# Layer 3's attention: five VectorE exponential tiles a block instead of four, the block's end in five pieces, and statistics' steps placed anew

## The chip, the cores and the metric

The kernel is one launch on one core of a Trainium2 chip. The metric is the device time in microseconds of that core; the median of the runs shown stands for a kernel. The engines are named PE (TensorE), DVE (VectorE), ACT (ScalarE), POOL (GpSimd) and SP (the queue that issues DMAs). [...]

## The reference

Four layers are applied to an image `x` of shape (2, 128, 64, 64), each to a group-normalised copy and added back: `x = x + layer(_gn(x))`. Layer 0 is an attention with four heads and depthwise convolutions, layer 1 a set of convolutions with a correlation, layer 2 a product of spectra (a two-dimensional real FFT, a quaternion product with weights per frequency, the inverse FFT). Layer 3, in which most of the change lies, is a plain attention of 8 heads with 16 channels each over 4096 positions:

```python
q = proj(wq, bq); k = proj(wk, bk); v = proj(wv, bv)      # (B, 8, 16, 4096)
a = jnp.einsum('bhcq,bhck->bhqk', q, k) / jnp.sqrt(jnp.float32(C))
a = jax.nn.softmax(a, axis=-1)
o = jnp.einsum('bhqk,bhck->bhcq', a, v)
```

All of it is computed in fp32.

## The kernel before

**Layer 3.** The work is cut into four groups: two images, and for each two sets of four heads (`b`, `t`). A group has eight blocks of 512 queries (`qb`), and a block has 32 iterations, one for each tile of 128 keys (`kt`). An iteration (`scores`) writes the scores of four heads by PE (L2316) into two PSUM tiles of [128, 2, 512], one for each pair of heads (`p` is 0 or 1). These come from a pool of three, two banks each[...]. One exponential instruction turns a PSUM tile into a tile of weights in SBUF: usually ACT's (L2330). For the tiles named in `BY_VECTOR`, DVE computes the exponential itself, with a chain of eight instructions (`exponentials`): `exp_i` reads the scores (L2272), two integer steps split exponent and mantissa (L2277, L2280), four terms of a polynomial (L2288) and the last term with the power of two make the weights (L2292). The chain is a generator, and the loop advances it by one piece an iteration, ahead of that iteration's scores, so DVE's order is fixed by the loop.

The products with the values (`multiply`, L2339) follow three iterations behind the scores (`LAG`), so those of a block's last key tile are issued in iteration 2 of the next block. `ORDER` says at which place of the sum each key tile is multiplied: a tile of DVE's comes some places later than its own. After the last one, `done` ends the block on DVE: a transpose of the accumulator (L2362), reciprocals of the sums (L2366), the product (L2367), a transpose back (L2369), the sum with the residual (L2370) and the stores.

While a group runs, the keys, queries and values of the next are made in the same loop (`queries_and_keys` in four pieces at the iterations of `KEYS`, `values` at iteration `VALUES`). In a usual block of the first three groups this is one chunk of queries and keys and one of values: PE's matmuls are L2197 and L2243, DVE's parts L2200 to L2223 and L2250. A group that is behind catches up at `MORE_KEYS`. Small steps (`bound`, the statistics of the next image, `folded`) stand at the iterations of `SMALL`. In the very first block of the layer, the first group's own keys and values are made, a chunk at every second iteration.

`_in_order` keeps each engine's instructions in program order. The tile framework assigns the buffers of a pool and places the semaphores.

**Statistics.** `_stats_steps` computes the group statistics of an image in eleven steps: eight `bn_stats` on DVE (L1444), their aggregation (L1447), a small matmul with the mean and three short DVE instructions (L1450 to L1459), and a small matmul with the variance, ended by a power on POOL (L1462, L1429, L1430). Layer 1 takes them in turn with its last chunks, each of which has a matmul series (L710), a sum (L721) and some of the DVE taps (L662). Layer 2 takes them in its last stage (`turned_back`, `added`; L1158 to L1175).

**Layer 2's start.** `placed` spreads the transformed rows of an image over the partitions (`copied`, L960 on ACT and L962 on DVE; even rows by ACT, odd rows by DVE). The second half of the weights' product (L1024) needs all rows of the mirrored part.

Of the kernel before, what the change touches and what calls it, by code (L numbers as in the profile page):

```python
# [18 lines left out]
CH = 512  # L19
# [512 lines left out]
def _layer1(ctx, tc, X, a, cst, here=None, there=None, consts=None):  # L532
# [216 lines left out]
    for b in range(B):  # L749
        for c in range(NCH):  # L750
            if c in (0, 2):
                z = on_tiles(g[b], t2[b], c // 2)
            ps = combined(t9[b], t2[b], c)

            for x in ready:
                added(*x)
            ready = [(b, c * CH, ps)]
            if c in (1, 3):
                ready.append((b, c // 2 * S // 2, z))
            some(rest, (4, 2, 4, 2, 3, 2, 2, 2)[c])  # L760
            some(steps, 2)
        if there is not None and b == 0:
            for x in ready:
                added(*x)
            ready = []
            steps = _stats_steps(nc, two, bank, X[:, 0, :], cst, mhalf, there)
# [36 lines left out]
def _layer2(ctx, tc, X, weights, cst, src, here=None, there=None, beside=None):  # L803
# [26 lines left out]
    with tc.tile_pool(name="l2_a", reuse_waits="tile", bufs=3) as ap, tc.tile_pool(  # L830
# [23 lines left out]
        scales = [st]  # L854
        shifts = [shifted(st)]
        if B > 1:
# [53 lines left out]
    with tc.tile_pool(name="l2_e", reuse_waits="tile", bufs=4) as ep, tc.tile_pool(  # L910
# [34 lines left out]

        def placed(kb, m, got, image, e, scalar):

            row = (m - 1) % 4  # L950
            s, row = (1, 3 - row) if image else (0, row)

            def copied(r, p, n=1):
                to = slice(32 * p, 32 * p + 32 * n)
                of = slice(32 * (r ^ p), 32 * (r ^ p) + 32 * n)
                sign = signs if n == 4 else float(SIGN2[r][p])
                out = e[to, row, :, 4 * r : 4 * r + 4].rearrange("p f (b c) -> p b f c", c=2)
                sign = sign[to, :] if n == 4 else sign
                if scalar:
                    nc.scalar.mul(out, got[of, :, s], sign)  # L960
                else:
                    nc.vector.tensor_scalar_mul(out, got[of, :, s], sign)  # L962

            copied(0, 0, 4)
            copied(2, 2, 2)
            copied(2, 0)
            copied(2, 1)
            yield
            for r in (1, 3):
                for p in range(4):  # L970
                    copied(r, p)
                yield
# [9 lines left out]

        def rows_in(kb, rows, places, es):

# [3 lines left out]
            yield  # L988
            yield from copies(kb, rows, gots, places, es)

        def copies(kb, rows, gots, places, es):
            for image in places:
                if es[image] is None:
                    es[image] = ep.tile([128, 4, 2 * PAIRS, 8 * B], F32, tag="e", name="e")
                yield from together(
                    *(
                        placed(kb, m, got, image, es[image], i % 2 == 0)
                        for i, (m, got) in enumerate(zip(rows, gots))
# [116 lines left out]
        for kb in range(BLOCKS2):  # L1115
# [10 lines left out]
            else:  # L1126
                later = side
                side, n = [copies(0, first[:2], gots[:2], (1,), e), rows_in(0, first[2:], (1,), e)], 8
            alongside(
# [18 lines left out]
    with tc.tile_pool(name="l2_c", reuse_waits="tile", bufs=3) as cp, tc.tile_pool(  # L1148
        name="l2_cps", reuse_waits="tile", bufs=4, space=PSUM
    ) as cps:  # L1150
        for b in range(B):
            xi = X[:, b, :].rearrange("p (h w) -> p h w", w=W)

            def turned_back(i):
                pt = cps.tile([128, CH], F32, tag="pt", name="ps_pt")
                for n in range(4):
# [5 lines left out]
                    )  # L1162
                for _ in range(2):
                    next(steps, None)
# [166 lines left out]
SMALL = (7, 9, 13, 15, 24, 28)  # L1331
BY_VECTOR = {(5, 1): 11, (12, 1): 18, (20, 1): 26, (27, 1): 31}

# [805 lines left out]
def _layer3(ctx, tc, X, l3, cst, out, worst, here, dram):  # L2139
# [129 lines left out]
    def exponentials(ps, out):  # L2269
# [17 lines left out]
        for n in EXP_TERMS[:-1]:  # L2287
            nc.vector.scalar_tensor_tensor(z, x, n, m, ALU.add, ALU.mult)  # L2288
            x = z
            yield  # L2290
        w = pp.tile([128, 2, CH], F32, tag="weights", name="weights")
# [6 lines left out]
    class Group:  # L2298

        def __init__(self, b, t, f, idle=0):  # L2300
            self.b, self.t, self.f, self.ac = b, t, f, None
            self.kept, self.q, self.k = {}, {}, {}
            self.vt = two.tile([128, NQT, 2, 3, 16], F32, tag="vt", name="vt")
# [4 lines left out]

    chain = [iter(())]

    def scores(g, qb, kt):
# [11 lines left out]
        for p in range(2):  # L2323
            g.weights[qb, kt, p] = w = []
            if (kt, p) in BY_VECTOR:
                chain[0] = exponentials(ps[p], w)
# [5 lines left out]
    def multiply(g, qb, at):  # L2332
        if at == 0:
            g.ac = acc()
        for j in range(4):

            i, kt = j % 2, ORDER[j // 2][at]
            (w,) = g.weights[qb, kt, j // 2]
# [7 lines left out]
        if at == NQT - 1:  # L2346
            done(g.b, g.t, qb, g.ac)

    def done(b, t, qb, ps):
# [12 lines left out]
        nc.vector.transpose(flat, ps)  # L2362
        r = two.tile([128, CH // 32], F32, tag="r", name="r")
        for j in range(4):
            rows = slice(32 * j, 32 * j + 32)
            nc.vector.reciprocal(r[rows, :], z[rows, :, 16 * (1 - j % 2)])  # L2366
        nc.vector.tensor_mul(z, z, r.unsqueeze(2).to_broadcast([128, CH // 32, 32]))  # L2367
        u = two.tile([128, CH], F32, tag="u", name="u", bufs=1)
        nc.vector.transpose(u, flat)  # L2369
        nc.vector.tensor_add(u, u, xs)  # L2370
        for at, rows in places:
            nc.sync.dma_start(out[b, rows, cols], u[at, :])

    def in_turn(*gens):
# [26 lines left out]
    def attended(g, early, others, following):  # L2401
# [19 lines left out]
        for n in range(NCH * NQT):  # L2421
# [3 lines left out]
            next(chain[0], None)  # L2425
            scores(g, qb, kt)
            waiting.append((g, qb, kt))
            if len(waiting) > LAG:
# [62 lines left out]
    for x in waiting:  # L2491
        multiply(*x)


# [32 lines left out]
def kernel(ctx, tc, a, out):  # L2527
# [4 lines left out]
    with tc.tile_pool(name="keep", bufs=1) as keep:  # L2532
        X, cst, eps5 = _inputs(tc, keep, a)

        worst = keep.tile([128, 1 + 2 * B], F32, name="worst")
        st = keep.tile([128, B + 2, 2], F32, name="st")
        rows_of_weights = _layer0(tc, X, a, cst, worst, st[:, :B], dram)
# [86 lines left out]
```

## Time and profile before

| | us |
|---|---|
| median of 3 runs | 4001.92 (4000.72 to 4008.1) |
| the profiled execution | 4003.18 |
| its span, first to last instruction | 4001.4 |
| busy PE / DVE / ACT in the span | 3853.4 / 3200.6 / 3243.5 |
| first scores of layer 3 | 2133.3 |

The page gives busy time, the span in slices, DMA, the chain that ended last, and groups of instructions as `line engine op out<-in xcount | busy, mean ns | idle before, releaser`. A timeline line is `start, length, engine, line, op, tiles`, with the idle time ahead of it and what ended that in brackets. Instructions on ACT and DVE overlap their neighbours a little, so a mean length is more than the distance of two starts; the ends of matmuls are modelled. Layer 3 takes 1867 us of the span, from 2133 to its end.

### The profile page before, as it was taken

What the parts mean: (1) busy time and instruction counts of PE and PEld (TensorE: products, weight loads), DVE (VectorE), ACT (ScalarE), POOL (GpSimd) and SP (SyncE); (2) the same over time, 40 slices, a digit from 0 to 9 for tenths busy, and PEclk for the clock granted to TensorE, in tenths of its full rate; (3) what the DMA queues carried; (4) which work ended last, traced back from release to release, by engine and by line L of the source; (5) the groups of instructions that cost most, each with busy time, mean ns of one, the idle gap of its engine ahead of it and who ended that gap; (6) DMA issues with size and microseconds to landing.
All of it is one profiled execution on the core that took longest, in us unless ns stands there. A gap on an engine that the chain in (4) does not pass through costs nothing.

```text
span 4001.4 us, 82144 instructions
## 1 busy us (share of the span) xinstructions
PE 3853.4 (96%) x35202; PEld 1313.9 (33%) x35202; DVE 3200.6 (80%) x3577; ACT 3243.5 (81%) x3948; POOL 86.2 (2%) x145
## 2 busy tenths in 40 slices
PE   7999999989999998998998999999999999999998
PEld 4511221353111124446664232232233222322222
DVE  6599999858999998996758777777777777776666
ACT  4499999736899983226645999999999999999998
POOL 1000000000000001000000000000000000000000
PEclk9999999999999999999998999999999999999999
DMA  1199960000000000004744110110002000110000
GB/s 51 23 200 185 187 106 2 1 2 2 2 2 2 2 2 13 6 19 199 280 199 150 32 32 25 53 46 31 26 27 72 30 27 25 44 47 6 6 6 5
DMA packets 193128, 217.59 MB, mean 54 GB/s; under 512 B 30441, under 2 KB 154345, under 8 KB 188658
## 3 DMA queue, kind: packets, MB, share of 16 engines
q1 hardware_dynamic: 192754, 212.25, 20.5%
q8 instruction: 278, 4.55, 0.5%
q14 instruction: 96, 0.79, 0.1%
HBM read 178.64 MB, written 98.57 MB: 69 GB/s over the span
## 4 chain that ended last, share of the span: by engine, by line
PE 78%; DVE 10%; issue 4%; ACT 2%; POOL 0%; SPq 0%; DMA 0%; ACTq 0%; POOLq 0%; DVEq 0%
PE ps_acc L2339 25%; PE ps_s L2316 19%; PE ps L1884 11%; PE ps L1892 11%; DVE X L662 3%; PE ps_z L1024 2%; PE ps_bank L710 2%; DVE sums L1915 2%; PE ps L1645 2%; DVE e L962 1%; PE ps_bank L681 1%; PE ps_bank L1078 1%; PE ps_acc L2197 1%; PE ps_acc L2243 1%; PE ps_pe L937 1%
## 5 line engine op out<-in xcount | busy, mean ns | idle before, releaser
L2330 ACT ACTIVATE weights<-ps_s 128x1024 f32<-128x1024 f32 x1920 | 1781.3, 1062 | 75.6 <-PE ps_s L2316 75.4
L2339 PE MATMUL ps_acc<-weights,vt 128*32 128x512 f32 x8192 | 1092.9, 605 | 0.0
L1915 DVE TENSOR_TENSOR sums<-sums,weights 128x2048 f32<-128x2048 f32 x384 | 854.2, 2283 | 3.5 <-ACT weights L1967 1.4
L2316 PE MATMUL ps_s<-q,k 64*128 64x512 f32 x4096 | 830.3, 469 | 3.7 <-DMA k<-stack 2.4
L1967 ACT ACTIVATE weights<-ps 128x1536 f32<-128x1536 f32 x512 | 740.6, 1447 | 6.9 <-PE ps L1892 6.9
L2316 PEld LDWEIGHTS ps_s<-q,k 64*128 64x128 f32 x4096 | 348.3, 184 | 935.2 <-ACT weights L2330 808.8
L1892 PE MATMUL ps<-q,k 32*64 32x512 f32 x8192 | 574.0, 612 | 3.6 <-ACT weights L1964 3.0
L1884 PE MATMUL ps<-weights,vt 128*32 128x512 f32 x4096 | 544.7, 604 | 0.0
L2288 DVE SCALAR_TENSOR_TENSOR exp_z<-exp_z,exp_m 128x1024 f32<-128x1024 f32 x384 | 469.0, 1221 | 9.3
L1964 ACT ACTIVATE weights<-ps 128x512 f32<-128x512 f32 x512 | 306.8, 599 | 75.3 <-PE ps L1892 36.5
L2272 DVE TENSOR_SCALAR exp_i<-ps_s 128x1024 int32<-128x1024 f32 x128 | 156.7, 1224 | 216.7 <-PE ps_s L2316 216.5
L2339 PEld LDWEIGHTS ps_acc<-weights,vt 128*32 128x32 f32 x8192 | 161.9, 108 | 309.6 <-issue 308.8
L1892 PEld LDWEIGHTS ps<-q,k 32*64 32x64 f32 x8192 | 120.0, 129 | 432.2 <-ACT weights L1964 381.7
L1884 PEld LDWEIGHTS ps<-weights,vt 128*32 128x32 f32 x4096 | 84.2, 108 | 390.9 <-issue 378.5
L662 DVE SCALAR_TENSOR_TENSOR X<-g,w,X 128x2048 f32<-128x2048 f32 x84 | 197.4, 2351 | 2.6
L2292 DVE SCALAR_TENSOR_TENSOR weights<-exp_z,exp_i 128x1024 f32<-128x1024 f32 x128 | 156.8, 1225 | 15.5 <-ACT weights L2330 0.5
L1915 DVE TENSOR_TENSOR sums<-weights 128x2048 f32<-128x2048 f32 x64 | 145.8, 2288 | 28.7 <-ACT weights L1967 27.9
L1645 PE MATMUL ps<-pad,diag 32*32 32x512 f32 x4032 | 151.8, 614 | 8.7 <-DVE qk L1656 4.1
L2288 DVE SCALAR_TENSOR_TENSOR exp_z<-exp_m 128x1024 f32<-128x1024 f32 x128 | 155.9, 1218 | 0.0
L1024 PE MATMUL ps_z<-w_ri,e 128*32 128x128 f32 x2048 | 142.9, 408 | 12.5 <-DVE e L962 6.9
L1645 PEld LDWEIGHTS ps<-pad,diag 32*32 32x32 f32 x4032 | 86.1, 104 | 69.3 <-issue 21.1
L962 DVE TENSOR_SCALAR e<-ps_pe 32x136 f32<-32x136 f32 (+1 forms) x341 | 101.1, 297 | 4.8
(321 smaller groups left out, 2943.0 us busy)
## 6 DMA issues: line engine op xcount, KB each, us to landing
w_ri<-w_r SPq DMA_DIRECT2D x16, 2112.0 KB, 8.1
w_ri<-w_i SPq DMA_DIRECT2D x16, 2112.0 KB, 13.0
stack<-qs SPq DMA_DIRECT2D x64, 256.0 KB, 2.1
q<-stack SPq DMA_DIRECT2D x128, 128.0 KB, 2.5
k<-stack SPq DMA_DIRECT2D x128, 128.0 KB, 2.6
stack<-ks SPq DMA_DIRECT2D x32, 256.0 KB, 2.1
w_r<-in_L_conv_kr_w SPq DMA_DIRECT2D x15, 528.0 KB, 12.6
w_r<-in_L_conv_kr_x SPq DMA_DIRECT2D x15, 528.0 KB, 12.6
```

The source lines that it names most:

```text
L662: nc.vector.scalar_tensor_tensor(xi, g[:, i : i + H // 2, j : j + W], w8[:, s : s + 1], xi, ALU.mult, ALU.add)
L1024: nc.tensor.matmul(out.rearrange("p (n f o) -> p n f o", n=2, f=2), e[:, s, 2 * j : 2 * j + 2, :].rearrange("p f x -> p (f x)"), w.rearran ...
L1645: nc.tensor.matmul(ps[r // 2][to, r % 2, :].rearrange("p (h w) -> p h w", w=W), diag[rows, grp, t, :], pad[rows, y0 : y0 + ROWS, t % 3 : t ...
L1884: nc.tensor.matmul(out[rows, :], lhs(rows), w[:, j, :], start=first, stop=stop)
L1892: nc.tensor.matmul(bank[64 * h : 64 * h + 64, :], k1[rows, kt * 128 + 64 * h : kt * 128 + 64 * h + 64], q1[rows, qb * CH : (qb + 1) * CH], ...
L1915: nc.vector.tensor_add(parts[p].rearrange("p j c -> p (j c)"), t.rearrange("p j c -> p (j c)"), w.rearrange("p j c -> p (j c)"),)
L1964: nc.scalar.activation(held[n][:, 0, :], single, AF.Exp)
L1967: nc.scalar.activation(held[n][:, 1:, :], three, AF.Exp)
L2288: nc.vector.scalar_tensor_tensor(z, x, n, m, ALU.add, ALU.mult)
L2316: nc.tensor.matmul(ps[j // 2][:, j % 2, :], g.k[kt // 4][rows, j // 2, keys], g.q[qb][rows, j // 2, :], start=True, stop=True,)
L2330: nc.scalar.activation(w[0], ps[p], AF.Exp)
L2339: nc.tensor.matmul(g.ac[32 * j : 32 * j + 32, :], g.vt[:, kt, j // 2, i : i + 2, :].rearrange("p a d -> p (a d)"), w[:, i, :], start=(at = ...
```

## The change

In layer 3, the tiles that DVE computes are now five a block, all of pair 0, at iterations 0, 6, 12, 20 and 26; they were four of pair 1. The chain's last two terms are one piece, so that it has six pieces, and its weights are multiplied at places 6, 12, 18, 26 and 31. The first block of the layer (a group whose `idle` is over 0) leaves all its tiles to ACT, and multiplies in plain order. The end of a block is a generator of five pieces, one an iteration: transpose; reciprocals (two over all partitions with every second column of a pair, in place of four over 32 partitions); product; transpose; sum and stores.

In layer 1 and in layer 2's last stage, the statistics' steps are taken two at a time for four chunks and then one at a time, and in layer 1 ahead of the chunk's taps. The product of negated mean and scale, which layer 2 computed at its start, is made in layer 1's last chunk. In layer 2's first block, the copies of rows 1 and 3 in the odd row of the last two go to ACT.

```diff
--- before.py
+++ after.py
@@ -757,8 +757,12 @@
             ready = [(b, c * CH, ps)]
             if c in (1, 3):
                 ready.append((b, c // 2 * S // 2, z))
+            some(steps, (2, 2, 2, 2, 1, 1, 1, 0)[c])
+            if there is not None and b == B - 1 and c == NCH - 1:
+                nc.vector.scalar_tensor_tensor(
+                    there[:, 2:3], there[:, 0:1], -1.0, there[:, 1:2], ALU.mult, ALU.mult
+                )
             some(rest, (4, 2, 4, 2, 3, 2, 2, 2)[c])
-            some(steps, 2)
         if there is not None and b == 0:
             for x in ready:
                 added(*x)
@@ -852,7 +856,7 @@
             return shift
 
         scales = [st]
-        shifts = [shifted(st)]
+        shifts = [shifted(st) if here is None else here[:, 2:3]]
         if B > 1:
             scales.append(ap.tile([128, 2], F32, tag="st", name="st"))
             steps = stats(1, scales[1])
@@ -943,7 +947,7 @@
                 )
             return pe[:, : B * 8 * PAIRS].rearrange("p (b s f c) -> p b s f c", b=B, s=2, c=2)
 
-        def placed(kb, m, got, image, e, scalar):
+        def placed(kb, m, got, image, e, scalar, helped=False):
 
 
 
@@ -966,6 +970,7 @@
             copied(2, 0)
             copied(2, 1)
             yield
+            scalar = scalar or helped
             for r in (1, 3):
                 for p in range(4):
                     copied(r, p)
@@ -980,21 +985,21 @@
                         gens.remove(g)
                 yield
 
-        def rows_in(kb, rows, places, es):
+        def rows_in(kb, rows, places, es, helped=False):
 
             yts = [transposed(m) for m in rows]
             yield
             gots = [transformed(m, yt) for m, yt in zip(rows, yts)]
             yield
-            yield from copies(kb, rows, gots, places, es)
-
-        def copies(kb, rows, gots, places, es):
+            yield from copies(kb, rows, gots, places, es, helped)
+
+        def copies(kb, rows, gots, places, es, helped=False):
             for image in places:
                 if es[image] is None:
                     es[image] = ep.tile([128, 4, 2 * PAIRS, 8 * B], F32, tag="e", name="e")
                 yield from together(
                     *(
-                        placed(kb, m, got, image, es[image], i % 2 == 0)
+                        placed(kb, m, got, image, es[image], i % 2 == 0, helped)
                         for i, (m, got) in enumerate(zip(rows, gots))
                     )
                 )
@@ -1125,7 +1130,7 @@
                 n += 6
             else:
                 later = side
-                side, n = [copies(0, first[:2], gots[:2], (1,), e), rows_in(0, first[2:], (1,), e)], 8
+                side, n = [copies(0, first[:2], gots[:2], (1,), e), rows_in(0, first[2:], (1,), e, True)], 8
             alongside(
                 products(rows_of_weights(kb, False), e[0], pzs[0], kb == 0),
                 chain(*side),
@@ -1160,7 +1165,7 @@
                         y[:, b, w : w + 2, :, :].rearrange("p w c f -> p (w c f)"),
                         ident,
                     )
-                for _ in range(2):
+                for _ in range((2, 2, 2, 2, 1, 1, 1, 0)[i]):
                     next(steps, None)
                 zt = cp.tile([128, CH], F32, name="zt")
                 nc.scalar.copy(zt, pt)
@@ -1329,7 +1334,7 @@
 KEYS, MORE_KEYS = (8, 16, 19, 23), (10, 14, 25, 29)
 VALUES, MORE_VALUES = 30, 22
 SMALL = (7, 9, 13, 15, 24, 28)
-BY_VECTOR = {(5, 1): 11, (12, 1): 18, (20, 1): 26, (27, 1): 31}
+BY_VECTOR = {(0, 0): 6, (6, 0): 12, (12, 0): 18, (20, 0): 26, (26, 0): 31}
 
 
 def _order(pair):
@@ -2287,7 +2292,8 @@
         for n in EXP_TERMS[:-1]:
             nc.vector.scalar_tensor_tensor(z, x, n, m, ALU.add, ALU.mult)
             x = z
-            yield
+            if n != EXP_TERMS[-2]:
+                yield
         w = pp.tile([128, 2, CH], F32, tag="weights", name="weights")
         nc.vector.scalar_tensor_tensor(
             w.rearrange("p j c -> p (j c)"), z, EXP_TERMS[-1], power, ALU.add, ALU.mult
@@ -2299,6 +2305,7 @@
 
         def __init__(self, b, t, f, idle=0):
             self.b, self.t, self.f, self.ac = b, t, f, None
+            self.busy = idle > 0
             self.kept, self.q, self.k = {}, {}, {}
             self.vt = two.tile([128, NQT, 2, 3, 16], F32, tag="vt", name="vt")
             self.top = two.tile([128, 2, NCH], F32, tag="top", name="top")
@@ -2307,6 +2314,7 @@
             self.weights = {}
 
     chain = [iter(())]
+    ending = [iter(())]
 
     def scores(g, qb, kt):
         ps = [spp.tile([128, 2, CH], F32, tag="sp", name="ps_s") for _ in range(2)]
@@ -2322,7 +2330,7 @@
             )
         for p in range(2):
             g.weights[qb, kt, p] = w = []
-            if (kt, p) in BY_VECTOR:
+            if (kt, p) in BY_VECTOR and not (g.busy and qb == 0):
                 chain[0] = exponentials(ps[p], w)
                 next(chain[0])
             else:
@@ -2334,7 +2342,7 @@
             g.ac = acc()
         for j in range(4):
 
-            i, kt = j % 2, ORDER[j // 2][at]
+            i, kt = j % 2, at if g.busy and qb == 0 else ORDER[j // 2][at]
             (w,) = g.weights[qb, kt, j // 2]
             nc.tensor.matmul(
                 g.ac[32 * j : 32 * j + 32, :],
@@ -2344,7 +2352,8 @@
                 stop=(at == NQT - 1),
             )
         if at == NQT - 1:
-            done(g.b, g.t, qb, g.ac)
+            ending[0] = done(g.b, g.t, qb, g.ac)
+            next(ending[0])
 
     def done(b, t, qb, ps):
         cols = slice(qb * CH, (qb + 1) * CH)
@@ -2360,16 +2369,23 @@
         z = two.tile([128, CH // 32, 32], F32, tag="z", name="z", bufs=1)
         flat = z.rearrange("p n i -> p (n i)")
         nc.vector.transpose(flat, ps)
-        r = two.tile([128, CH // 32], F32, tag="r", name="r")
-        for j in range(4):
-            rows = slice(32 * j, 32 * j + 32)
-            nc.vector.reciprocal(r[rows, :], z[rows, :, 16 * (1 - j % 2)])
-        nc.vector.tensor_mul(z, z, r.unsqueeze(2).to_broadcast([128, CH // 32, 32]))
+        yield
+        r = two.tile([128, CH // 32, 2], F32, tag="r", name="r")
+        for h in range(2):
+            nc.vector.reciprocal(r[:, :, h], z[:, :, 16 * (1 - h)])
+        yield
+        halves = z.rearrange("p n (h i) -> p n h i", h=2)
+        nc.vector.tensor_mul(
+            halves, halves, r.unsqueeze(3).to_broadcast([128, CH // 32, 2, 16])
+        )
+        yield
         u = two.tile([128, CH], F32, tag="u", name="u", bufs=1)
         nc.vector.transpose(u, flat)
+        yield
         nc.vector.tensor_add(u, u, xs)
         for at, rows in places:
             nc.sync.dma_start(out[b, rows, cols], u[at, :])
+        yield
 
     def in_turn(*gens):
         gens = list(gens)
@@ -2424,6 +2440,7 @@
                 over = next(early, early) is early
             next(chain[0], None)
             scores(g, qb, kt)
+            next(ending[0], None)
             waiting.append((g, qb, kt))
             if len(waiting) > LAG:
                 multiply(*waiting.pop(0))
@@ -2490,6 +2507,7 @@
     run(chain[0])
     for x in waiting:
         multiply(*x)
+    run(ending[0])
 
 
 def _input(nc, X, a, b):
@@ -2533,7 +2551,7 @@
         X, cst, eps5 = _inputs(tc, keep, a)
 
         worst = keep.tile([128, 1 + 2 * B], F32, name="worst")
-        st = keep.tile([128, B + 2, 2], F32, name="st")
+        st = keep.tile([128, B + 2, 3], F32, name="st")
         rows_of_weights = _layer0(tc, X, a, cst, worst, st[:, :B], dram)
         with tc.tile_pool(name="late", reuse_waits="tile", bufs=1) as late:
             with tc.tile_pool(name="raw", reuse_waits="tile", bufs=1) as raw:
```

## The prediction

> **What bounds the kernel now.** I read the busy slices of the page first: from slice 22 on, ACT and PE both stand at 9. A busy PE is no limit by itself (matmul ends are modelled), so I took the groups: L2330, the exponentials by ScalarE, waits only 75.4 us for PE in all, and L2316's weight loads wait 808.8 us for those exponentials.
>
> ```profile
> L2330 ACT ACTIVATE weights<-ps_s 128x1024 f32<-128x1024 f32 x1920 | 1781.3, 1062 | 75.6 <-PE ps_s L2316 75.4
> L2316 PEld LDWEIGHTS ps_s<-q,k 64*128 64x128 f32 x4096 | 348.3, 184 | 935.2 <-ACT weights L2330 808.8
> ```
>
> Then ScalarE's own timeline, first a block of the last group (no projections beside it), then one of the second group:
>
> ```profile
> 3604.14 12.04 ACT L2330 ACTIVATE weights<-ps_s 128x1024 f32<-128x1024 f32 x13 [0.24 <-PE ps_s L2316]
> 3616.36 13.86 ACT L2330 ACTIVATE weights<-ps_s 128x1024 f32<-128x1024 f32 x15 [0.18 <-PE ps_s L2316]
> 3630.41 12.03 ACT L2330 ACTIVATE weights<-ps_s 128x1024 f32<-128x1024 f32 x13 [0.19 <-PE ps_s L2316]
> ```
> ```profile
> 2903.03 12.02 ACT L2330 ACTIVATE weights<-ps_s 128x1024 f32<-128x1024 f32 x13 [0.61 <-PE ps_s L2316]
> 2935.36 6.52 ACT L2330 ACTIVATE weights<-ps_s 128x1024 f32<-128x1024 f32 x7 [0.42 <-PE ps_s L2316]
> 2960.50 1.94 ACT L2330 ACTIVATE weights<-ps_s 128x1024 f32<-128x1024 f32 x2 [0.61 <-PE ps_s L2316]
> ```
>
> To be seen: ScalarE runs without a hole except once after each VectorE tile and once after each piece of projection. Starts inside a run are 0.905 to 0.92 us apart, so I use **0.908**. From 3616.36 to 3630.41 are 14.05 us for 15 tiles: 15 x 0.908 = 13.62, so a VectorE tile costs ScalarE 0.43 of idling. A block of the second group lasts 2960.50 - 2903.03 = 57.47 = 60 x 0.908 (54.5) + four such holes (1.66) + two projection holes (1.3). In the last group it is 54.5 + 4 x 0.43 = 56.2. PE alone could go faster: in the unhindered iterations the scores' starts are 1.656 apart, 53.0 a block, 55.1 with the two projections (1.06 each). So the attention is bound by ScalarE, with PE 1 to 3 us behind, and VectorE has room:
>
> ```profile
> 2904.14:2961.62 57.48, 57.48 (x400) 17.12 (x396) 43.79 (x53) 55.66 (x61) 0.00 (x0) 1.00 0.09 28
> ```
>
> (The columns are length, then busy PE, PEld, DVE, ACT, POOL.) VectorE has 43.8 us of 57.5.
>
> [...] the transpose L2362 holds VectorE 2.46 us for PE and nothing passes it. [...] here the end is broken up between instructions, and no run yet shows its worth.
>
> **The change, part by part.**
>
> *1. Fifth tile, blocks 1 to 31.* ScalarE loses one tile (-0.908) and gains one hole (+0.43): -0.48 a block. A tile frees 0.48 net, which PE-paced iterations eat at 2 x 0.908 - 1.656 = 0.16 each, so three of them; the new distances are 6, 6, 8, 6, 6, long enough. Only the first tile comes two iterations after the projection hole at kt 30: +0.1 there. Sum: 23 blocks x -0.38 = **-8.7**; last eight x -0.48 = **-3.8**.
>
> *2. VectorE's added work, and who queues behind it.* A chain is 1.22 + 2 x 0.69 + 5 x 1.22 = 8.7, with gaps 8.9. Five are 44.5; the end of a block 3.97 (transpose to sum, 2966.80 on), now 3.4 since two reciprocals of 0.245 go; one chunk of queries and keys 5.0; values 0.5. That is 53.4 of about 57: it fits, barely, and not evenly. Between kt 2 and kt 6 the order is transpose 0.72, term 1.22, reciprocals 0.49, term 1.22, product 0.69, two terms 2.45, transpose 0.71, and then exp_i of tile 6. The sum is 7.5 from the end of PE's products of kt 2, some 7.1 with the 0.08 by which independent instructions overlap. The scores of tile 6 are there 5.8 after that moment (three iterations of 1.7 to 1.8, and 0.54), so exp_i comes 1.3 to 1.7, I take **1.4, late**. From it to exp_i of tile 12 are 10.5 (8.9, the last sum, and the two reductions of kt 8) against 10.4 for six iterations: still 1.5 late. At kt 16 VectorE waits for PE's projection and is level again at 20. The values' sum at kt 30 starts as iteration 31 does, 3.1 before exp_i of the next tile 0, which is due after 2.2: 0.9 late. Late tiles hold a score buffer. In a pair, the third score after one is only 1.65 us away, so a fixed rotation of three buffers would make PE wait. The trace says that the rotation isn't fixed: in the first block exp_i ran late, and the scores three tiles later did not wait for it:
>
> ```profile
> 2149.35 1.21 DVE L2272 TENSOR_SCALAR exp_i<-ps_s 128x1024 int32<-128x1024 f32 x1
> 2149.97 0.18 PEld L2316 LDWEIGHTS ps_s<-q,k 64*128 64x128 f32 x2 [0.86 <-ACT weights L2330]
> ```
>
> A buffer that ScalarE frees was taken there. With that choice a lateness under 2.0 costs nothing, since two buffers carry PE for two iterations; I take 0 for it, and keep 2.3 a block as the upper end (rival A). The weights come in time: tile 6's are wanted at kt 15.
>
> *3. PE's own waits for VectorE.* Bound, statistics and the folding of the next image send PE small matmuls that need a VectorE result: about six per kernel between kt 7 and 15 of a block. Now VectorE is ahead; then 1.5 behind, and PE waits with the scores behind it: 6 x 1.4 = **+8**, from 0 to 15. The blocks that catch up eight pieces in one (group 0): **+3**, from 0 to 6.
>
> *4. First block by ScalarE.* It took 77.2 (first scores 2133.3, next block's 2210.5). PE's holes in it for VectorE (0.42, 0.66, 0.37, 1.37, 1.75, 2.85) are 7.4; VectorE has 35 us of chains there beside six chunks of keys. Without chains these go; the four tiles more lie under PE until kt 24, then eight iterations at 1.82 instead of 1.66 cost about 1. Sum **-7**, from -4 to -10.
>
> *5. Layer 1's statistics.* VectorE's taps (L662, 2.35 each) fill the end of that layer. VectorE idles 0.74 before L1455, and here:
>
> ```profile
> 1782.42 0.16 DVE L1429 TENSOR_SCALAR st<-ps_bank 128x1 f32<-128x1 f32 x1 [2.42 <-PE ps_bank L1462]
> ```
>
> With each step a chunk later and ahead of the taps, PE has 5 to 7 us of taps to answer in: **-3**, from -1 to -4. The negated mean moves before layer 2 (0.15, hidden by the last taps).
>
> *6. Layer 2.* Eight copies of 0.31 go from VectorE to ScalarE, which idles 7.14 before 1854.57 while PE waits for them:
>
> ```profile
> 1853.18 0.67 PE L1024 MATMUL ps_z<-w_ri,e 128*32 128x128 f32 x8 [3.31 <-issue]
> ```
>
> **-2.5**, between 0 (the weights' transfer next) and -3.3. The last stage's statistics, one step a tile from the aggregation on, let PE pass on from the hole of 2.47 before L1450 at 2110.39: **-1.2**, between +1 and -2. The last block's end has two reciprocals less: **-0.5**. No DMA is added; the residual loads are issued as before, the outputs four iterations later, 30 before the next use.
>
> Sum: -8.7 - 3.8 + 8 + 3 - 7 - 3 - 2.5 - 1.2 - 0.5 = **-15.7**. The profiled execution took 4003.2 (span 4001.4), 1.3 above the median of 4001.9. On the median: 3986, given as **3985**.
>
> **Rivals.** *A, slower: the late VectorE tile stops PE.* If the scores of kt+1's second pair take the very buffer that the VectorE tile holds, PE waits from a lateness of 0.36 on. At 1.4, PE stops about 1.05 and ScalarE loses 0.9; at tile 12 1.0, at tile 0 0.4. That is +2.3 in 23 blocks and +0.9 in eight: +60, so 4046; with tile 6 alone 31 x 0.9 = +28, so 4014. For it: the steady blocks of before reuse the VectorE buffer three tiles later each time. Against: there VectorE was early, and in the first block it was passed over. *B, faster: the price of a tile is less and VectorE's waits for PE shrink instead of growing.* No part 3, and the full 0.91 for a tile: 31 x -0.43 - 11 = -24 more: 3962. For it: PE's floor leaves 2 us. Against: the hole after each VectorE tile is the same at four places. *C, the five tiles give nothing* (each freed tile is lost to VectorE's delay), and parts 4 to 6 alone remain: -14 + 11 = about no change, 3999.
>
> **How the numbers follow.** Forecast 0.50 (3972 to 3997), A 0.25 (3998 to 4050), B 0.15 (3945 to 3972), C 0.10 (3990 to 4005). 0.2%, about what a measurement of this kernel tells from no change, is 8 us. Faster by more (under 3994): 0.44 + 0.15 + 0.04 = 0.63; within: 0.06 + 0.03 + 0.05 = 0.14; slower: 0.22 + 0.01 = 0.23. The range 3952 to 4035 leaves out the ends of A and B.
>
> **What would show it.** Right: blocks of 57.1 in groups 0 to 2, 55.8 in the last; five holes of about 0.43 on ScalarE; first block about 70; L2272 no longer idle before tiles 6 and 12. Wrong: L2316's weight loads waiting for VectorE by more than 0.84 each, holes over 1 us on ScalarE at kt 7 and 13 (A), or blocks near 56 (B).

## The result, and the profile after

The changed kernel is slower: a median of 4032.7 us (4029.1 to 4036.8, four runs) beside 4005.0 for the kernel before in the same series. The ratio is 1.0069, with a 95% interval from 1.0058 to 1.0081. The profiled execution of after has a span of 4027.0, that of before 4001.4: +25.6, where the forecast summed to -15.7.

First the groups of the page that answer to those shown of before (columns: busy time and mean ns of one; idle time of the engine ahead of them, and what ended most of it).

```profile
L2338 ACT ACTIVATE weights<-ps_s 128x1024 f32<-128x1024 f32 x1893 | 1769.9, 1057 | 117.1 <-PE ps_s L2324 114.9
L2324 PE MATMUL ps_s<-q,k 64*128 64x512 f32 x4096 | 823.4, 467 | 39.0 <-DVE exp_i L2277 35.8
L2277 DVE TENSOR_SCALAR exp_i<-ps_s 128x1024 int32<-128x1024 f32 x155 | 188.6, 1217 | 96.5 <-PE ps_s L2324 90.9
```

ScalarE has 27 tiles fewer, and yet it waits 117.1 us for PE in place of 75.6. The second line says why: PE itself now sits idle for 35.8 us until VectorE's `exp_i` is through. Before, the idle time ahead of this group was 3.7 in all, and most of it was for a transfer:

```profile
L2316 PE MATMUL ps_s<-q,k 64*128 64x512 f32 x4096 | 830.3, 469 | 3.7 <-DMA k<-stack 2.4
```

Next ScalarE's timeline of a block in the second group of after, and then part of a block in the last group.

```profile
2911.84 2.92 ACT L2338 ACTIVATE weights<-ps_s 128x1024 f32<-128x1024 f32 x3 [0.40 <-PE ps_s L2324]
2915.16 2.15 ACT L2338 ACTIVATE weights<-ps_s 128x1024 f32<-128x1024 f32 x2 [0.40 <-PE ps_s L2324]
2917.77 8.36 ACT L2338 ACTIVATE weights<-ps_s 128x1024 f32<-128x1024 f32 x9 [0.46 <-PE ps_s L2324]
2926.39 10.19 ACT L2338 ACTIVATE weights<-ps_s 128x1024 f32<-128x1024 f32 x11 [0.26 <-PE ps_s L2324]
2936.82 1.03 ACT L2338 ACTIVATE weights<-ps_s 128x1024 f32<-128x1024 f32 x1 [0.24 <-PE ps_s L2324]
2938.06 1.02 ACT L2338 ACTIVATE weights<-ps_s 128x1024 f32<-128x1024 f32 x1 [0.22 <-PE ps_s L2324]
2939.55 5.60 ACT L2338 ACTIVATE weights<-ps_s 128x1024 f32<-128x1024 f32 x6 [0.46 <-PE ps_s L2324]
```
```profile
3614.25 10.19 ACT L2338 ACTIVATE weights<-ps_s 128x1024 f32<-128x1024 f32 x11 [0.24 <-PE ps_s L2324]
3624.69 10.19 ACT L2338 ACTIVATE weights<-ps_s 128x1024 f32<-128x1024 f32 x11 [0.25 <-PE ps_s L2324]
```

In the last group there is one hole per VectorE tile and nothing else. Tile 6 of the second group is the same (2926.39). But after tile 0 (2915.16) and after tile 12 (2936.82) come second and third holes, ending at 2917.77 and at 2938.06 and 2939.55. These are the loss: beyond the 0.908 from start to start, and beyond the one hole of each tile, key tile 1 costs ScalarE 0.81 and key tile 13 costs it 0.90 (medians of the blocks 1 to 7 of the groups 1 and 2).

PE's timeline at these two places, and then the chain of waits through the first of them (start, length, what):

```profile
2914.56 0.50 PE L2324 MATMUL ps_s<-q,k 64*128 64x512 f32 x2
2915.75 0.49 PE L2324 MATMUL ps_s<-q,k 64*128 64x512 f32 x2 [0.70 <-DVE exp_i L2277]
```
```profile
2936.21 0.50 PE L2324 MATMUL ps_s<-q,k 64*128 64x512 f32 x2
2937.51 0.51 PE L2324 MATMUL ps_s<-q,k 64*128 64x512 f32 x2 [0.80 <-DVE exp_i L2277]
```
```profile
2911.35 0.56 DVE vt L2255
...
2913.14 1.24 DVE weights L2298
...
2914.47 1.24 DVE exp_i L2277
2915.71 0.04 issue
2915.75 0.49 PE ps_s L2324 x2
```

In key tiles 1 and 13 the first pair's scores go, and the second pair's stop until VectorE has read the tile before. The chain now runs through VectorE: values' sum, rest of the old tile, `exp_i` of tile 0, and only then PE.

The balance from the starts of the blocks of layer 3, after less before: first scores -2.6; first block of the layer -9.9 (77.2 to 67.3); blocks 1 to 7 of group 0 +13.0; first blocks of groups 1 to 3 +10.3; the fourteen other blocks of groups 1 and 2 +18.7 (57.48 to 58.78 is the usual one); those of the last group -2.5 (56.24 to 55.86). That sums to +27.1 at the last scores, and +25.6 at the end.

VectorE is busy for 50.9 of such a block's 58.8 us, so it has 8 us left:

```profile
2912.90:2971.68 58.78, 57.28 (x399) 17.17 (x395) 50.87 (x59) 55.32 (x60) 0.00 (x0) 1.00 0.09 28
```

### The profile page after: what moved, and what is told of

It reads as the page before. It is cut to its first block, busy times and chain, and to the rows that moved or that the text cites. A ratio compares the mean times of both kernels' runs of the same rounds, so it can differ in the third digit from the quotient of the medians.

```text
span 4027.0 us, 82289 instructions
## 1 busy us (share of the span) xinstructions
PE 3848.1 (96%) x35202; PEld 1318.9 (33%) x35202; DVE 3383.8 (84%) x3721; ACT 3234.3 (80%) x3929; POOL 88.3 (2%) x145
## 4 chain that ended last, share of the span: by engine, by line
PE 77%; DVE 11%; issue 4%; ACT 3%; POOL 0%; DMA 0%; SPq 0%; DVEq 0%; POOLq 0%; ACTq 0%
PE ps_acc L2347 23%; PE ps_s L2324 17%; PE ps L1889 11%; PE ps L1897 11%; PE ps_bank L710 2%; PE ps_z L1029 2%; DVE sums L1920 2%; PE ps L1650 2%; DVE exp_i L2277 1%; DVE weights L2298 1%; PE ps_t L640 1%; DVE e L966 1%; DVE exp_z L2293 1%; PE ps_bank L590 1%; PE ps_bank L1083 1%
## 5 line engine op out<-in xcount | busy, mean ns | idle before, releaser
L2338 ACT ACTIVATE weights<-ps_s 128x1024 f32<-128x1024 f32 x1893 | 1769.9, 1057 | 117.1 <-PE ps_s L2324 114.9
L2324 PE MATMUL ps_s<-q,k 64*128 64x512 f32 x4096 | 823.4, 467 | 39.0 <-DVE exp_i L2277 35.8
L2293 DVE SCALAR_TENSOR_TENSOR exp_z<-exp_z,exp_m 128x1024 f32<-128x1024 f32 x465 | 565.0, 1215 | 9.2
L2277 DVE TENSOR_SCALAR exp_i<-ps_s 128x1024 int32<-128x1024 f32 x155 | 188.6, 1217 | 96.5 <-PE ps_s L2324 90.9
L2298 DVE SCALAR_TENSOR_TENSOR weights<-exp_z,exp_i 128x1024 f32<-128x1024 f32 x155 | 189.9, 1225 | 16.6 <-DVE exp_z L2293 0.5
L2293 DVE SCALAR_TENSOR_TENSOR exp_z<-exp_m 128x1024 f32<-128x1024 f32 x155 | 188.8, 1218 | 0.0
L2285 DVE TENSOR_SCALAR exp_i<-exp_i 128x1024 int32<-128x1024 int32 x155 | 107.6, 694 | 5.3
L2282 DVE TENSOR_SCALAR exp_m<-exp_i 128x1024 int32<-128x1024 int32 x155 | 107.2, 692 | 4.3
```

The source lines that it names most:

```text
L2277: nc.vector.tensor_scalar(i, ps.rearrange("p j c -> p (j c)"), EXP_SCALE, EXP_BIAS, ALU.mult, ALU.add)
L2298: nc.vector.scalar_tensor_tensor(w.rearrange("p j c -> p (j c)"), z, EXP_TERMS[-1], power, ALU.add, ALU.mult)
L2324: nc.tensor.matmul(ps[j // 2][:, j % 2, :], g.k[kt // 4][rows, j // 2, keys], g.q[qb][rows, j // 2, :], start=True, stop=True,)
L2338: nc.scalar.activation(w[0], ps[p], AF.Exp)
```

## The experiments

**Theory T.** VectorE comes about 1 us late to tiles 0 and 12, because of the values' sum and the two reductions queued ahead of them. In this order of program the buffer of a VectorE tile of the first pair goes to the scores that come third after it, which are the second ones of the next key tile, and PE stops. **Rival R:** five tiles are simply too much work for VectorE, wherever its pieces lie. **Rival R2:** another part of the change (the end in pieces, the first block) costs the time.

How late a tile is can be read from the trace: an `exp_i` on time starts 0.54 after the second matmul of its scores starts. In the groups 1 and 2 of after, the means are 1.59 for tile 0, 1.73 for tile 6, 1.85 for tile 12, and 0.54 for tiles 20 and 26. Late are thus tile 0 by 1.05, tile 6 by 1.2, tile 12 by 1.3.

Who takes a buffer can be read too, from the semaphore that the weight load of each pair's scores waits for: ScalarE's or VectorE's. In these blocks of after, the scores that come third wait for VectorE behind the tiles 0, 12, 20 and 26; behind tile 6 it is the fourth ones. This half of theory T is thus seen in the trace, and it says why tile 6 is late without a stop.

### One cause of lateness at a time

```diff
-VALUES, MORE_VALUES = 30, 22
+VALUES, MORE_VALUES = 14, 22
```

> The kernel after with one number changed: the values' projection of a block is issued at key tile 14, where VectorE waits for PE anyway, and no longer at 30. Theory T: VectorE is about 1 us late at the tiles 0 and 12, the buffer that it holds is the one that the second scores of the next key tile take, and PE stops there. Then the stop at key tile 1 goes and the one at 13 stays: ScalarE's loss at key tile 1 falls from 0.52 + 0.58 to about 0.45, blocks of groups 0 to 2 from 58.78 to 58.0 (57.9 to 58.3), the time from 4032.7 to about 4015. Rival R (VectorE has simply too much to do with five tiles, wherever its pieces lie): blocks stay at 58.8 and the time at 4030 to 4035, with the loss moved to another key tile.

Measured: 4012.7, ratio 1.0019 (1.0011 to 1.0027). Tile 0 is on time (0.54), key tile 1 is back at 1.66, and the blocks are 58.18. The stop at 13 remains, and the projection costs 0.89 at its new place, more than the 0.58 of the old; that is why the blocks are not 58.0. PE's wait for `exp_i` halves:

```profile
L2324 PE MATMUL ps_s<-q,k 64*128 64x512 f32 x4096 | 829.3, 469 | 20.8 <-DVE exp_i L2277 17.8
```

```diff
-KEYS, MORE_KEYS = (8, 16, 19, 23), (10, 14, 25, 29)
+KEYS, MORE_KEYS = (29, 16, 19, 23), (10, 14, 25, 29)
```

> The kernel after with one number changed: the two reductions of a chunk (1.15 us of VectorE) come at key tile 29 of the same block, in VectorE's wait for the values, and no longer at 8 of the next one. Theory T: tile 12 is then late by 0.3 to 0.4 in place of 1.2 to 1.5, the stop at key tile 13 goes or falls under 0.1, the one at 1 stays. Blocks from 58.78 to about 57.95 (57.8 to 58.3), time about 4014. Rival R (too much work for VectorE in sum): the blocks stay at 58.8.

Measured: 4013.3, ratio 1.0023 (1.0014 to 1.0033). Tile 12 is late by 0.24, key tile 13 takes 1.66 to 1.70, blocks of groups 1 and 2 are 57.86. In group 0 the gain is missing (58.7 to 59.0): there the pieces run in other places, and tiles 20 and 26 are late by 0.85 in turn.

Both edits together:

> The kernel after with both moves at once (values at key tile 14, reductions at 29), tiles in the first pair. Theory T: the two stops have separate causes, so the gains add: blocks of groups 0 to 2 at 57.3 (57.2 to 57.6), no scores waiting for VectorE by more than 0.1 but in the first blocks of the groups, time 3994 to 4000. Rival (one stop only takes the lateness off the next tile; with neither, VectorE is late elsewhere): blocks of 57.9 or more, time of 4008 or more.

Measured: 3998.3, ratio 0.9987 (0.9979 to 0.9995); blocks of groups 1 and 2 at 57.26, with tiles 0, 12, 20 and 26 late by 0.08 at most and tile 6 still by 1.0. PE's wait for `exp_i` falls to 8.0:

```profile
L2324 PE MATMUL ps_s<-q,k 64*128 64x512 f32 x4096 | 825.7, 468 | 11.3 <-DVE exp_i L2277 8.0
```

The two stops have separate causes: in these blocks the gains of 0.60 and 0.92 add to 1.52. In group 0, where tiles 20 and 26 are late as with the one edit, blocks take 57.9 and not the 57.3 expected. VectorE does the same work in after and in these three kernels, so rival R falls: it is the place of the work.

### The same lateness, another distance

```diff
-BY_VECTOR = {(0, 0): 6, (6, 0): 12, (12, 0): 18, (20, 0): 26, (26, 0): 31}
+BY_VECTOR = {(0, 1): 6, (6, 1): 12, (12, 1): 18, (20, 1): 26, (26, 1): 31}
```

> The kernel after with the five tiles of VectorE taken from the second pair, nothing else moved: VectorE does the same work in the same order. A tile's scores are then ready 0.43 later and its buffer is taken by the first scores two key tiles on, 0.8 later than before, so about 1.2 us more lateness is allowed. Theory T: no scores wait for VectorE by more than 0.1 us, blocks of groups 0 to 2 come to 57.1 (57.0 to 57.3), the last group stays at 55.9, the time falls by 23 x 1.65 + 2 to 3992 (3988 to 3998). Rival R (too much work for VectorE): blocks stay at 58.8, time 4030 to 4035, since VectorE's work is unchanged.

Measured: 3988.5, ratio 0.9964 (0.9952 to 0.9977); blocks 57.0 and 55.57. VectorE's order is untouched and tile 12 is still late by 1.1, but nobody waits for it: the buffer is now wanted 1.49 after an `exp_i` that is on time is through, where it was 0.41 in the first pair. A part of the gain is the pair itself: in the last group, where no scores wait for VectorE in either kernel, a block takes 55.57 with the second pair and 55.86 with the first, since the hole after each tile is shorter by some 0.06. PE's page line of this kernel, and ScalarE in a block of its second group:

```profile
L2324 PE MATMUL ps_s<-q,k 64*128 64x512 f32 x4096 | 813.6, 465 | 7.4 <-DVE exp_i L2277 4.5
```
```profile
2896.33 10.19 ACT L2338 ACTIVATE weights<-ps_s 128x1024 f32<-128x1024 f32 x11 [0.40 <-PE ps_s L2324]
2906.71 10.20 ACT L2338 ACTIVATE weights<-ps_s 128x1024 f32<-128x1024 f32 x11 [0.19 <-PE ps_s L2324]
```

Apart from the projections, the holes are one per tile again.

### The dose

The kernel with the five tiles in the second pair, and in addition:

```diff
-        for n, x in enumerate((q[0], k)):
+        for n, x in 2 * tuple(enumerate((q[0], k))):
```

> The kernel with the five tiles in the second pair (nothing else moved from after), and the two reductions of a chunk issued twice, with the same result: 1.2 us more for VectorE just ahead of tile 12, nothing more for PE or ScalarE. It takes the dose of lateness and looks for the point from which it costs. In the second pair tile 12 is now 1.1 late and its buffer is wanted 1.49 after an exponential that is on time is through; so 1.1 costs nothing and 2.3 should stop PE by 2.3 - 1.44 = 0.85. Theory T: a new stop at key tile 14 in groups 0 to 2, blocks of 57.8 to 58.0 there and 55.6 in the last group (no chunks of keys there), time 3988.5 + 23 x 0.9 = 4009 (4003 to 4014). Rival (VectorE's lateness as such is harmless in the second pair, since PE takes another buffer): blocks stay at 57.0, 3985 to 3993.

Measured: 4012.8, ratio 1.0017 (1.0011 to 1.0024); blocks 57.84 in groups 0 to 2, 55.57 in the last. Tile 12 is late by 2.28, and PE stops:

```profile
2927.68 1.07 PE L2347 MATMUL ps_acc<-weights,vt 128*32 128x512 f32 x8
2929.52 0.73 PE L2324 MATMUL ps_s<-q,k 64*128 64x512 f32 x4 [0.77 <-DVE exp_i L2277]
```

So lateness costs nothing up to the distance, and about one for one beyond it (the distance of 1.49 less the 0.05 from the end of `exp_i` to the scores is 1.44; 2.28 - 1.44 = 0.84, and ScalarE loses 0.84). The 1.2 us themselves would have found room: VectorE has 6 to 8 us left in a block.

### The other parts of the change

Four tiles a block, in the old places, all else as in after:

```diff
-BY_VECTOR = {(0, 0): 6, (6, 0): 12, (12, 0): 18, (20, 0): 26, (26, 0): 31}
+BY_VECTOR = {(5, 1): 11, (12, 1): 18, (20, 1): 26, (27, 1): 31}
```

> The kernel after with the four tiles a block of the kernel before (second pair, key tiles 5, 12, 20, 27), all other parts of the change kept. Theory T: only the fifth tile and its places cost; blocks are the 57.48 and 56.24 of before, and what is left is the gain of the first block (9.9), of the start of layer 3 (2.6) and of the last block's end (0.5): 4005.0 - 13 = 3992 (3988 to 3998). Rival R2 (the block's end in five pieces or the first block by ScalarE delays something in the blocks after): blocks of 57.8 or more and a time of 4000 or more.

Measured: 3992.8, ratio 0.9972 (0.9961 to 0.9983); blocks 57.50 and 56.25, those of before within 0.03. R2 falls for these blocks: their loss lies with the fifth tile and the new places. Only the first blocks of groups 1 to 3 take 0.9 more each than before (59.55, 58.53 and 56.94 for 58.64, 57.61 and 56.02), 2.7 in all, and this belongs to some other part of the change. The run also gives the price of a fifth tile when nothing stops: 57.50 to 57.01, and 56.25 to 55.57 in the last group.

The end of a block in one piece, tiles as in after:

```diff
-            ending[0] = done(g.b, g.t, qb, g.ac)
-            next(ending[0])
+            run(done(g.b, g.t, qb, g.ac))
```

> The kernel after with the end of a block issued in one piece again (transpose, both reciprocals, product, transpose, sum at once after the products of key tile 2); tiles as in after. Theory T: VectorE's order puts the sum (0.67) ahead of the exponentials of tile 6 too, so this tile is late by 2.0, and in this order of program the second scores of key tile 7 take the buffer of tile 6: PE stops there by about 1.5, ScalarE loses 1.4 at key tile 7. Tile 12 is then late by 0.3 less or more and its stop shrinks. Blocks of groups 0 to 2: 59.4 (59.0 to 60.2); blocks of the last group 56.9 in place of 55.9; time about 4055 (4043 to 4070). Rival R3 (the pieces serve nothing, as the one piece did no harm with four tiles): 58.8, 55.9 and 4030 to 4035.

Measured: 4115.3, ratio 1.0282 (1.0266 to 1.0298); blocks 61.6, and 58.1 to 59.4 in the last group. The direction is as expected and the size is not. Tile 6 is late by 2.82, not 2.0, and PE stops for 2.31. From the transpose to `exp_i` of tile 6 are 8.34 us here (2948.43 to 2956.77) and 6.71 in after (2918.97 to 2925.68). The sum, which now runs ahead of the tile, is 0.67 of this difference. The rest fits the gaps, though no run takes it apart: in one piece the steps depend on each other and start 0.03 to 0.04 after one another's end, while interleaved with the chain they overlap by 0.06 to 0.1. Then a second thing happened, seen in the windows (length; busy PE, PEld, DVE, ACT, POOL; granted TensorE clock; DMA):

```profile
2957.00:2958.00 1.00, 0.00 (x0) 0.00 (x0) 1.00 (x1) 0.00 (x0) 0.00 (x0) 1.00 0.00 0
2958.00:2959.00 1.00, 0.95 (x10) 0.34 (x10) 0.94 (x2) 0.40 (x1) 0.00 (x0) 1.00 0.00 0
2959.00:2960.00 1.00, 1.00 (x10) 0.27 (x4) 1.00 (x2) 0.62 (x1) 0.00 (x0) 0.58 0.00 0
2960.00:2961.00 1.00, 1.00 (x8) 0.35 (x12) 1.00 (x2) 0.37 (x1) 0.00 (x0) 0.50 0.00 0
2961.00:2962.00 1.00, 1.00 (x8) 0.08 (x8) 1.00 (x3) 1.00 (x2) 0.00 (x0) 0.50 0.00 0
2962.00:2963.00 1.00, 1.00 (x6) 0.30 (x4) 0.97 (x2) 0.57 (x1) 0.00 (x0) 0.71 0.00 0
```

A microsecond after PE has resumed, its clock is granted at half, for 3.4 us, and key tile 8 takes 2.96 in place of 1.66. Key tiles 7 to 9 of this block take 9.10 together. In two blocks of group 0 a stop of the same length left the clock at 1.00, and they take 7.56 and 7.88. So a stop of 2.3 costs ScalarE 3.8 to 4.0 on average in groups 1 and 2, where stops of 0.7 and 0.8 cost 0.81 and 0.90.

### PE's own small products

The kernel with the five tiles in the second pair, and in `folded` (after `means`) and in `bound` (after `mm`):

```diff
+        yield
         ps = acc()
```

> The kernel with the five tiles in the second pair, and in addition the bound and the folding of the next image each cut in two steps: VectorE's part is issued one step (two to four key tiles) ahead of PE's small matmul that needs it. Part 3 of the prediction (PE's own waits for a late VectorE) is put to the test. Theory T: in the first blocks of the groups 1 to 3 key tile 7 takes 4.5 to 4.7 us in place of 2.0 because the bound's matmul waits for two reductions behind the exponentials' chain; this falls to 2.3 or less, and the first blocks from 64.1, 61.3 and 59.7 to 59, 58 and 57. The time goes from 3988.5 to about 3978 (3974 to 3984). Rival (those 2.5 us are VectorE's own work in that block, and come back at the next tiles): the first blocks lose less than 1 us each, and the time stays over 3985.

Measured: 3978.1, ratio 0.9935 (0.9921 to 0.9948). The first blocks of groups 1 to 3 fall to 58.9, 57.5 and 55.9. Group 1's first block without the edit, and then with it:

```profile
2615.13 1.06 PE L2347 MATMUL ps_acc<-weights,vt 128*32 128x512 f32 x8
2618.47 0.59 PE L2269 MATMUL ps_acc<-mm,head_sum 128*128 128x1 f32 x2 [2.28 <-DVE mm L2267]
2618.99 1.22 PE L2324 MATMUL ps_s<-q,k 64*128 64x512 f32 x4
```
```profile
2612.65 1.07 PE L2349 MATMUL ps_acc<-weights,vt 128*32 128x512 f32 x8
2613.73 0.73 PE L2326 MATMUL ps_s<-q,k 64*128 64x512 f32 x4
```

So the 2.5 us were no work of VectorE's that comes back later. A matmul of 128x1 had held PE for 2.28 us, and here too the next scores ran at half the clock (1.22 where 0.73 is usual; the granted clock is 0.59 from 2618 to 2620 and 0.50 from there to 2624). This version beats both kernels: it keeps all parts of the change.

### Layers 1 and 2

The kernel before with only these parts of the change (its core below), and then the best version with only these parts undone:

```diff
+            some(steps, (2, 2, 2, 2, 1, 1, 1, 0)[c])
...
             some(rest, (4, 2, 4, 2, 3, 2, 2, 2)[c])
-            some(steps, 2)
...
+            scalar = scalar or helped
...
-                for _ in range(2):
+                for _ in range((2, 2, 2, 2, 1, 1, 1, 0)[i]):
                     next(steps, None)
```

> The kernel before with the parts of the change that lie in the layers 1 and 2 alone (statistics' steps ahead of the taps, negated mean beforehand, eight copies by ScalarE, the last stage's statistics regrouped); layer 3 as before. The prediction gave it -3, -2.5 and -1.2, so -6.7. Theory T1: that holds, layer 2 starts 3.3 earlier and layer 3's first scores come 6 to 7 earlier; in the profile of after they came only 2.6 earlier because PE was granted a lower clock in a stretch of layer 2. Theory T2: layer 2 is paced by something that gives the lead of the eight copies back, and layer 3 starts 3 to 4 earlier, ratio 0.9990 to 0.9993.

And for the best version without these parts:

> The kernel with the five tiles in the second pair and the small products a step later (3978.1, ratio 0.9935), but with the layers 1 and 2 of before. The parts 5 and 6 of the prediction (-3, -2.5, -1.2) taken by themselves a second time, from the other side. Theory T1: they are worth the 6.7 forecast: ratio 0.9952, about 3985. Theory T2: they are worth next to nothing in the time of the runs, as where they were alone: ratio 0.9930 to 0.9940, about 3978.

Measured: alone 4003.0, ratio 0.9997 (0.9989 to 1.0006). Without them the best version is at 3983.6, ratio 0.9941 (0.9928 to 0.9955) beside 0.9935 with them. The idle times that the prediction named did shrink in the profile of after: ahead of the statistics from 2.42 to 0.33, and ahead of the weights' product from 3.31 to 1.43.

```profile
1781.04 0.16 DVE L1434 TENSOR_SCALAR st<-ps_bank 128x1 f32<-128x1 f32 x1 [0.33 <-PE ps_bank L1467]
```
```profile
1847.98 0.65 PE L1029 MATMUL ps_z<-w_ri,e 128*32 128x128 f32 x8 [1.43 <-ACT e L964]
```

The lower clock that theory T1 of the first of the two runs names is in the profiles: from 1850 to 1900 it was 0.80 in after, 0.90 before and 0.86 with these parts alone; that it held the first scores back was not shown. And the first scores of layer 3 vary by more than the gain between profiled executions of equal code up to there: 2126.8 to 2135.0 with these parts, 2133.3 and 2141.8 without. Nine of the ten with them come before both without, which speaks for a gain; the medians of the runs show none where the parts stand alone, and bound it at some 4.4 us. Whether there is any is not settled.

## Why the prediction was wrong, by its own steps

- **Part 1, the price of a tile: right.** A hole of 0.43 was forecast; it is 0.42 to 0.52 in the first pair. The fifth tile alone brings -0.49 a block (second pair), where -0.38 was forecast. In the last group, where -0.48 was, it brings -0.68 in the second pair and -0.38 in the first.
- **Part 2, how late VectorE is: right.** Forecast 0.9, 1.4 and 1.5 for tiles 0, 6 and 12, and level again at 20; measured 1.05, 1.2, 1.3 and 0.
- **Part 2, "a lateness under 2.0 costs nothing, since two buffers carry PE for two iterations": this is the step that failed.** It holds for tile 6, whose buffer goes to the fourth scores after it, and not for tiles 0 and 12: there the third scores take the very buffer. Taken as zero, it costs 0.81 + 0.90 in each of some 23 blocks, about +39, nearly all of the miss of 41. The evidence was weighed wrongly. The prediction had both sides, for under rival A it says that the steady blocks of before reuse VectorE's buffer three tiles later each time; it set this aside because VectorE was early there, and took one late tile of the first block for the rule. The steady blocks are this line of who waited for whom in the profile of before:

```profile
PEld ps_s L2316 <- DVE exp_m L2277: 104.0, 124, 0.8
```

  It has 124 weight loads of scores released by VectorE (the view names `exp_m`, which follows `exp_i` there), with 128 VectorE tiles in the kernel. Their 0.84 each is no loss, since loads released by ScalarE show the same 0.84 of idle time; the line tells only whose buffer is taken. By the semaphores, 125 of the 128 buffers went to the third scores. The other three are tiles 5, 12 and 20 of the first block, late by 2.9 to 5.7. So the first block was the exception. Nor does lateness alone decide it: tile 6 of after, late by 1.2, is passed over once, tiles 0 and 12 beside it are not, and with the end in one piece tile 6 is late by 2.82 and is not. What does decide it, no run here shows.
- **Rival A is what happened**, with its threshold right (stops from a lateness of 0.36; an `exp_i` on time leaves 0.41) and one of its signs too (46 weight loads waited 52.7 us for `exp_i`, 1.15 each). Its places are right for two of three: it had ScalarE lose 0.4 at tile 0, 0.9 at tile 6 and 1.0 at tile 12, and tile 6 also in the last group; measured are 0.81, nothing and 0.90. Its 4046 compares with 4033.
- **Part 3: right in size, in part by luck.** The first blocks of groups 1 to 3 lost 10.3, or 8 more than the blocks around them changed; +8 was forecast. It came from fewer places, above all the bound's matmul, with 6.4 us of PE in three waits, and 2.7 stands with four tiles too. Catching up in group 0 cost about 4, where 3 was forecast.
- **Part 4: -9.9 for -7**, inside its range of -4 to -10. No run here takes the rest apart; with this part, the first block took 66.15 to 68.95 in the profiles, where before it took 77.17.
- **Parts 5 and 6: over-sized or unseen.** Sum -6.7 forecast; the holes closed by 2.1 and 1.9, the time gained is between none and 4.4.
- **Rivals B and C fall:** without the stops the usual blocks of groups 0 to 2 take 57.0, not B's 56, and five tiles are worth more than nothing (3988.5 against 3992.8 with four; in the profiles 0.5 a block).

With the failed step replaced, the forecast's sum is -15.7 + 39 = +23, measured +25.6. That it comes so near is partly luck: part 4 was 2.9 too small, the start of layer 3 came 4.1 less early than forecast, and the last group gained 1.3 less.

## What to carry to other kernels

A late engine off the critical path cost nothing here until the buffer it held was the next one wanted (a lateness of 0.36 in the first pair, 1.44 in the second), and about one for one after that (0.84 us lost for 0.84 beyond it), more where a stop of over 2 us brought the clock down to 0.50 (3.8 to 4.0 us lost for a stop of 2.3). So count the distance from the release to the reuse for every late tile, and count all the waits in the trace, not one of them. The distance is a cheap thing to change: taking the other pair of heads moved the ratio from 1.0069 to 0.9964, some 42 us, without touching any engine's work; about 9 us of it (31 blocks of 0.29) is that pair's shorter holes. Small products on PE that depend on a loaded engine are worth issuing a step after the work that they wait for: here this took another 10 us.

## What the runs showed of the hardware

- After PE stops of 2.1 to 3.0 us the granted clock often fell to 0.50, but not always. With the end in one piece it did after 25 of the 31 stops at key tile 7, and the mean granted clock of that profile is 0.976, where after has 0.986; after stops of the same 2.3, key tile 8 took anything from 1.66 to 3.02. In the profile of after, three stops ahead of the bound's matmul, of 2.15, 2.14 and 2.16, ended at 2632.67, 3105.71 and 3578.96: over the next 4 us the granted clock was 1.00 on average after the first, 0.57 after the second and 0.66 after the third. What decides it was not shown. Stops of 0.7 to 0.8 left the clock at 1.00.
- Two reciprocals over 128x16 take 0.36 together, where the kernel before had 0.245 for each of four over 32 partitions.
